# Moving the pieces of the range checks in the second layer of a two-layer attention kernel, and forming the verdict ahead of the last eviction

## The chip, the cores and the metric

The kernel runs as one program on one core of a Trainium2 chip. The metric is the device time of one execution in microseconds (us). Of the kernel before there are three timed runs and one further execution that the hardware profiler recorded.

## The reference, cut to what matters

The input x is an image of 128 rows, 256 columns and 256 channels in float32. Two layers are applied to it, each as a residual on top of a group norm. Layer 0 is a gated row attention with a pair bias. Layer 1, the only one that the change touches, is a banded attention along each row:

```
qkv = x2 @ w_in.T + b_in                       # x2: group norm of x, 128 rows of 256 x 256
scores = einsum('bhid,bhjd->bhij', q, k) / sqrt(64)          # 4 heads of 64
attn = softmax(where(|i - j| <= 16, scores, -inf))
out = einsum('bhij,bhjd->bhid', attn, v)
x = x + out @ w_out.T + b_out
```

The softmax of the kernel is computed without a subtraction of the row maximum: exponentials are summed, and the result is multiplied by the reciprocal of the sum. That is exact enough only while the sums stay in a safe range, so the kernel also looks at its sums, at the exponentials of the pair bias and at the mask, and sets a flag, the verdict. The engines then read the flag, and a slower general kernel would follow if it were set.

## The kernel before, in words

`mixer_kernel` calls `fast_kernel`, loads the verdict into a register of every engine (L2244) and branches on it (L2245). Everything below is the last part of `fast_kernel`, layer 1.

**Tiling.** 128 partitions; a row of the image is 256 positions, two blocks of 128 (NB = 2), and 256 channels are two blocks of 128 (KC = 2). The rows are handled two at a time in 64 objects of class `Pair1` (NP = 64). The order of instructions on every engine is the order in which the Python code is written, since all of it lies in `with tc.manual_schedule()`. Engines run in parallel and wait for one another by semaphores, so the order on each queue is what the change alters.

**The loop.** Iteration p of the loop over 63 pairs (L2115 and after) has four pairs in hand: `was` (pair p-1) is finished, `now` (pair p) goes through its attention, `nxt` (pair p+1) is projected, and `nn` and `n3` are loaded, transposed (`turn`, L1850), normalised (`centre`, L1855) and given the sums and differences of blocks that the projection uses (`differences`, L1868 to L1871, on POOL). The projection is a seven-product scheme: `product(n, i)` for n = 0, 1, 2 (query, key, value) issues the matmuls of product i (L1906, L1902 for the values) into one of two PSUM tiles x and y, ACT copies x to SBUF (L1915, L1913), and `join(n, i)` on DVE (L1922) adds y to that copy. A later product that writes y has to wait until the join before it has read y.

**The attention.** `scores` (PE L1959, ACT exponential L1968, POOL multiplication by the band mask L1970), `apply` (PE L1984 for the values, L1992 for the sums, into the PSUM tiles `o_eo` and `su_y`), `copy_sums` and `copy_odd` (ACT L2003, L2006), `join_sums` and `join_odd` (DVE L2009, L2012), `invert` (DVE reciprocal L2015), `weigh` (DVE L2020), `out_block` (PE L2038, eight matmuls for a row), and `keep_row` (DVE L2046, adds the residual and evicts from PSUM; then the store is issued on SP, L2052 or L2054). `out_row` is `out_block` for both blocks and then `keep_row`. The output tile `y` shares `su_y` with the sums, but for the last pair, where it has its own PSUM tile `ps_y1`.

**The range checks.** `look` puts two pieces on a list. The piece `low` is two DVE instructions, a comparison into the scratch tile `above` (tensor_scalar, L2071) and a minimum over it (tensor_reduce, L2072). The other piece is one DVE instruction, a maximum (tensor_reduce, L2074). `some_checks(n)` takes n pieces from the front of the list `late` if it has any, else of the list `checks`, and issues them at that place of DVE's queue. At p = 1 the list `checks` has 25 looks, that is 50 pieces (16 of the pair bias, one of the mask, eight of layer 0's sums). At p = 58 four looks more are put on it, of layer 1's sums of the first 56 pairs, the last of half width. Each of the last eight pairs (LATE = 8) puts its own two looks on `late` in `weigh`, one for each row.

Pieces are taken at these places of an iteration: **slot 1** after `was.invert(1)` (one piece if p > 0), the **centre slot** after `nn.centre(0)` (two if p > 56), **slot 2** after `now.join_odd(0)` (one if p > 0), and the **end slot** after `n3.turn()` (one if p > 56).

**The end.** After the loop, pair 62 is finished and pair 63 goes through its attention. Two pieces are taken after `now.weigh(0)` of pair 63, the rest at the very end after `now.out_row(1)`. Then follow a comparison of the maxima (`below`, L2081), the minimum over all results (L2231), a matmul with ones that adds it over the partitions (L2233), and the verdict (DVE, L2234).

Of the kernel before, what the change touches and what calls it, by code (L numbers as in the profile page):

```python
# [9 lines left out]
F32 = mybir.dt.float32  # L10
AF = mybir.ActivationFunctionType
ALU = mybir.AluOpType
AX = mybir.AxisListType
# [3 lines left out]
P = 128  # L17
# [756 lines left out]
def fast_kernel(  # L774
# [25 lines left out]
    nc = tc.nc  # L800
# [7 lines left out]
    NB = I // P  # L808
    KC = C // P
    NP = S // 2  # L810
# [10 lines left out]
    ones = const.tile([P, P], F32, name="ones")  # L821
# [109 lines left out]
    for a in range(KC):  # L931
        for h in range(H1):
            n = P // H1
# [5 lines left out]
    for h in range(H1):  # L939
        n = P // H1  # L940
# [10 lines left out]
    ok = const.tile([P, 2, 48], F32, name="ok")  # L951
# [596 lines left out]
    now = nxt = nn = None  # L1548
# [63 lines left out]
    behind, nx, n = None, 0, 0  # L1612
# [41 lines left out]
    with tc.manual_schedule():  # L1654
        old = was = Nobody()
        es = nn3 = None
        for p in range(NP):
# [71 lines left out]
            old, was, now, nxt, nn = was, now, nxt, nn, nn3  # L1729
# [39 lines left out]
    LATE = 8  # L1769
    rsum1 = dram.tile([NP, H1, 2, I], F32, name="rsum1")  # L1770
    with tc.tile_pool(name="l1", bufs=2) as sb, tc.tile_pool(
        name="l1s", bufs=4
    ) as sm, tc.tile_pool(name="ps1_s", bufs=2, space=PSUM) as ps_s, tc.tile_pool(
        name="ps1_o", bufs=1, space=PSUM
    ) as ps_o:

        def mm1(name, side=0):
            return ps_s.tile([P, 512], F32, name=name, tag=f"s{side}")
# [29 lines left out]
        def mix_weights():  # L1808

            a = [[w_in[:, k].rearrange("p (n m c) -> p m n c", n=3, m=KC)[:, m] for k in range(KC)]  # L1810
                 for m in range(KC)]
            s1, s2, s3, s4 = (wst[:, n] for n in range(4))
            nc.gpsimd.tensor_tensor(s1, a[1][0], a[1][1], ALU.add)
            nc.gpsimd.tensor_tensor(s2, s1, a[0][0], ALU.subtract)
            nc.gpsimd.tensor_tensor(s3, a[0][0], a[1][0], ALU.subtract)
            nc.gpsimd.tensor_tensor(s4, a[0][1], s2, ALU.subtract)
# [239 lines left out]
        def pair1(p):  # L2056
            return Pair1(p) if p < NP else Nobody()
# [6 lines left out]
        def look(queue, src, lo):  # L2064

            at = cols[0]
            cols[0] += 1

            def low():
                above = sm.tile([P, I], F32, name="above", tag="above", bufs=1)[:, : src.shape[1]]  # L2070
                nc.vector.tensor_scalar(above, src, lo, None, ALU.is_gt)  # L2071
                nc.vector.tensor_reduce(ok[:, 0, at : at + 1], above, AX.X, ALU.min)  # L2072

            queue += [low, lambda: nc.vector.tensor_reduce(ok[:, 1, at : at + 1], src, AX.X, ALU.max)]  # L2074

        def look_all(src, lo):
            for i in range(0, src.shape[1], I):
                look(checks, src[:, i : min(i + I, src.shape[1])], lo)
# [4 lines left out]
        def some_checks(n):  # L2083
            for _ in range(n):
                queue = late or checks
                if queue:
                    queue.pop(0)()

        def load_sums(src, name):
            t = sb.tile([P, src.shape[0] // P], F32, name=name, tag=name, bufs=1)  # L2090
            nc.sync.dma_start(t, src.rearrange("(a b) -> a b", a=P))
            look_all(t, 1e-16)

        with tc.manual_schedule():
            now, nxt = pair1(0), pair1(1)
            now.turn()
            norm1()
            mix_weights()
            for k in range(KC):
                now.centre(k)  # L2100
            nxt.turn()
            for m in range(KC):
                now.project("qT", m)
                now.project("kT", m)
                nxt.centre(m)
            nxt.differences()
            for r in range(2):
                now.values(r)
            now.add_bias()
            nxt.add_bias()  # L2110
            look_all(eb.rearrange("p h b i -> p (h b i)"), math.exp(-20.0))
            n_eb = cols[0]

            was = Nobody()
            for p in range(NP - 1):  # L2115
                nn = pair1(p + 2) if p == 0 else n3
                n3 = pair1(p + 3)
                if p == 0:
                    nn.turn()
                if p == 1:  # L2120
                    mask_t = sb.tile([S, I], F32, name="mask_all", bufs=1)
                    nc.sync.dma_start(mask_t, mask)
                    look_all(mask_t, 1e-15)
                    n_mask = cols[0]
                    load_sums(rsum.rearrange("n q r c i -> (n q r c i)"), "sums0")
                if p == NP - LATE + 2:
                    load_sums(rsum1[: NP - LATE].rearrange("n q r i -> (n q r i)"), "sums1")

                now.scores(0)
                now.scores(1)  # L2130
                was.apply(1)
                nxt.begin_fast()
                was.copy_sums(1)
                nxt.product(0, 1)
                was.copy_odd(1)
                nxt.product(1, 1)
                was.join_sums(1)
                for n in range(2):
                    nxt.product(n, 2)
                    nxt.join(n, 2)  # L2140
                was.invert(1)
                some_checks(p > 0)
                for i in (6, 5, 7):
                    for n in range(2):
                        nxt.product(n, i)
                for n in range(2):
                    nxt.join(n, 5)
                was.join_odd(1)
                was.weigh(1)
                was.out_row(0)  # L2150
                for n in range(2):
                    nxt.product(n, 4)
                    nxt.product(n, 3)
                    nxt.join(n, 3)
                fast = p < NP - 2
                if fast:
                    nxt.product(2, 1)
                    nxt.product(2, 2)
                    nxt.join(2, 2)
                nn.centre(0)  # L2160
                some_checks(2 if p > NP - LATE else 0)

                now.apply(0)
                now.copy_sums(0)
                if fast:
                    nxt.product(2, 6)
                    nxt.product(2, 5)
                now.copy_odd(0)
                now.join_sums(0)
                was.out_block(1, 0)  # L2170
                if fast:
                    nxt.product(2, 7)
                now.join_odd(0)
                some_checks(p > 0)
                was.out_block(1, 1)
                if fast:
                    nxt.join(2, 5)
                was.keep_row(1)
                if fast:
                    nxt.product(2, 4)  # L2180
                    nxt.product(2, 3)
                    nxt.join(2, 3)
                now.invert(0)
                now.weigh(0)
                nn.centre(1)
                nn.differences()
                nn.add_bias()
                n3.turn()
                some_checks(p > NP - LATE)
                if p == NP // 2:  # L2190
                    below(0, n_eb, math.exp(20.0))
                    below(n_eb, n_mask, 1e15)
                was, now, nxt = now, nxt, nn

            now.scores(0)
            was.apply(1)
            was.copy_sums(1)
            was.copy_odd(1)
            now.values(0)
            was.join_sums(1)  # L2200
            was.join_odd(1)
            was.invert(1)
            was.weigh(1)
            was.out_row(0)
            now.scores(1)
            now.values(1, 1)
            was.out_row(1)
            now.apply(0)
            now.copy_sums(0)
            now.copy_odd(0)  # L2210
            now.join_sums(0)
            now.join_odd(0)
            now.invert(0)
            now.weigh(0)
            some_checks(2)
            now.apply(1)
            now.copy_sums(1)
            now.copy_odd(1)
            for b in range(NB):
                now.out_block(0, b)  # L2220
            now.join_sums(1)
            now.invert(1)
            now.join_odd(1)
            now.weigh(1)
            now.keep_row(0)
            now.out_row(1)
            some_checks(len(checks) + len(late))
            below(n_mask, cols[0], 1e8)

        tot = sm.tile([P, 1], F32, name="okmin", bufs=1)  # L2230
        nc.vector.tensor_reduce(tot, ok.rearrange("p a n -> p (a n)"), AX.X, ALU.min)  # L2231
        ps = mm1("ok_ps")
        nc.tensor.matmul(ps[:, 0:1], ones, tot, start=True, stop=True)  # L2233
        nc.vector.tensor_scalar(verdict, ps[0:1, 0:1], P - 0.5, None, ALU.is_lt)  # L2234


# [63 lines left out]
```

## Time and profile before

| what | value |
|---|---|
| three timed runs | 3146.48, 3148.49, 3148.63 us (median 3148.49) |
| the profiled execution's own time | 3147.36 us |
| its span, first to last instruction | 3145.6 us |
| mean TensorE clock granted | 0.983 of full speed |
| busy share of the span | PE 96%, DVE 77%, POOL 72%, ACT 50% |
| layer 1's loop, first scores of p = 0 to first scores of p = 62 | 2007.19 to 3093.58 us |
| verdict written, span's end | 3139.03 us, 3145.6 us |

How to read the lines that follow: a line of the timeline gives the start in us from the span's beginning, the time from the start to the end of the merged instructions, the engine, the source line, the operation, output and inputs by the program's names, the shapes, how many instructions were merged, and in brackets how long the engine sat idle before and what ended that. PE is the matmul stream, PEld the weight loads beside it, SPq the queue of SyncE that issues DMAs.

### The profile page before, as it was taken

To read this page: it belongs to the slowest core of one execution; us is meant where nothing else is said; L and a number is where in the kernel's file an instruction comes from. 1 tells how busy PE (TensorE), PEld (TensorE's weight loads), DVE (VectorE), ACT (ScalarE), POOL (GpSimd) and SP (SyncE) were. 2 spreads that over 40 slices of the span, in tenths; PEclk is the share of its full clock that TensorE was granted. 3 is DMA by queue.
4 is the path that set the end of the run, shared out by engine and by line. 5 is a ranking of instruction groups with operands and counts; after the bars stand their busy time and mean duration, and the time that the engine had idled before them with its cause. 6 is when DMAs were issued, how large, how long until landed. Compare 5 with 4: busy or idle time off the path is not lost.

```text
span 3145.6 us, 80608 instructions
## 1 busy us (share of the span) xinstructions
PE 3020.1 (96%) x33630; PEld 2099.2 (67%) x33630; DVE 2406.7 (77%) x4007; ACT 1573.3 (50%) x2637; POOL 2270.8 (72%) x1633
## 2 busy tenths in 40 slices
PE   5679999999999999999999999899999999999997
PEld 3345555665555556655555565688888888888886
DVE  7976777777777777777777777688888777777787
ACT  3454444444444444444444444355555555555553
POOL 3459898898889988888899887455555555555552
PEclk9789999999999999999999999999999999999998
DMA  9952334323333343333333332534344444444441
GB/s 358 389 174 56 97 70 99 99 64 92 94 99 70 98 99 73 89 91 94 72 96 98 88 82 65 119 91 94 92 94 92 94 92 94 92 93 92 93 98 36
DMA packets 690951, 328.17 MB, mean 104 GB/s; under 512 B 538672, under 2 KB 639920, under 8 KB 689424
## 3 DMA queue, kind: packets, MB, share of 16 engines
q1 hardware_dynamic: 686176, 320.28, 39.5%
q8 instruction: 266, 4.36, 0.6%
q10 hardware_dynamic: 4400, 2.63, 0.3%
q14 instruction: 109, 0.89, 0.1%
HBM read 254.09 MB, written 68.75 MB: 103 GB/s over the span
## 4 chain that ended last, share of the span: by engine, by line
PE 84%; DVE 8%; DMA 2%; issue 2%; POOL 2%; ACT 1%; ACTq 0%; DVEq 0%; POOLq 0%; SPq 0%
PE ps_p L1347 21%; PE ps_sc L1384 8%; PE ps_qk L1906 8%; PE ps_ov L1419 7%; PE ps_y L1474 7%; PE ps_v L1365 7%; PE ps_qk L1902 7%; PE ps_su_y L2038 6%; PE ps_o L1984 3%; PE ps_su L1427 3%; PE ps_sc L1959 3%; PE ps_su_y L1992 2%; DVE rv L2015 2%; DMA xa<-in_x_dram 1%; DVE st L1182 1%
## 5 line engine op out<-in xcount | busy, mean ns | idle before, releaser
L1408 POOL TENSOR_TENSOR eboth<-e 128x512 f32<-128x512 f32 x512 | 745.0, 1476 | 177.3 <-PE ps_su L1427 96.2
L1404 DVE TENSOR_TENSOR e<-ps_sc,eb 128x1024 f32<-128x1024 f32 x384 | 458.4, 1221 | 289.3 <-ACT ps_sc L1396 289.2
L1396 ACT ACTIVATE ps_sc<-ps_sc 128x1024 f32<-128x1024 f32 x384 | 375.7, 1008 | 435.9 <-PE ps_sc L1384 309.7
L1384 PE MATMUL ps_sc<-qT,kT 32*128 32x256 f32 x4096 | 294.1, 400 | 0.9 <-DVE e L1404 0.9
L1869 POOL TENSOR_TENSOR dT<-xgT,dT 128x256 f32<-128x256 f32 x63 | 45.9, 729 | 317.4 <-ACT xgT L1855 317.4
L1970 POOL TENSOR_TENSOR e<-e,bw 128x384 f32<-128x384 f32 x256 | 249.5, 1003 | 11.3 <-ACT e L1968 11.3
L2038 PE MATMUL ps_su_y<-w_out,oT 128*128 128x256 f32 x1008 | 254.5, 385 | 1.8 <-DVE sums L2009 1.8
L1384 PEld LDWEIGHTS ps_sc<-qT,kT 32*128 32x128 f32 x4096 | 185.3, 184 | 103.0 <-issue 91.0
L1474 PEld LDWEIGHTS ps_y<-wo,oT 128*128 128x128 f32 x1024 | 194.1, 190 | 83.9 <-issue 44.5
L1347 PE MATMUL ps_p<-xnT,wq 128*128 128x512 f32 x512 | 247.6, 606 | 0.8 <-POOL xnT L1334 0.8
L1419 PE MATMUL ps_ov<-e,v 128*32 128x256 f32 x4096 | 247.6, 382 | 0.0
L1347 PE MATMUL ps_p<-xgT,wg 128*128 128x512 f32 x512 | 247.2, 605 | 0.1
L1474 PE MATMUL ps_y<-wo,oT 128*128 128x256 f32 x1024 | 242.3, 380 | 3.5 <-POOL oT L1464 2.7
L1365 PE MATMUL ps_v<-wv,xnT 128*128 128x256 f32 x1024 | 242.0, 379 | 1.6 <-ACT xgT L1316 1.6
L1347 PE MATMUL ps_p<-xnT,wk 128*128 128x512 f32 x512 | 240.6, 592 | 0.0
L1365 PEld LDWEIGHTS ps_v<-wv,xnT 128*128 128x128 f32 x1024 | 194.5, 190 | 55.9 <-issue 31.1
L1915 ACT ACTIVATE u<-ps_qk,bin_c 128x256 f32<-128x256 f32 x378 | 174.5, 476 | 102.2 <-PE ps_qk L1906 102.2
L2015 DVE RECIPROCAL rv<-sums 128x256 f32<-128x256 f32 x128 | 223.1, 1743 | 0.0
L2038 PEld LDWEIGHTS ps_su_y<-w_out,oT 128*128 128x128 f32 x1008 | 181.7, 190 | 23.6 <-DVE sums L2009 2.6
L1419 PEld LDWEIGHTS ps_ov<-e,v 128*32 128x32 f32 x4096 | 120.0, 109 | 108.4 <-issue 41.8
L1906 PE MATMUL ps_qk<-dT,wst 128*128 128x256 f32 x756 | 174.8, 380 | 7.1 <-DVE qT L1922 7.1
L1868 POOL TENSOR_TENSOR dT<-xgT 128x256 f32<-128x256 f32 x63 | 45.9, 729 | 186.0 <-ACT xgT L1855 186.0
(231 smaller groups left out, 6546.4 us busy)
## 6 DMA issues: line engine op xcount, KB each, us to landing
xa<-in_x_dram SPq DMA_DIRECT2D x8, 4096.0 KB
xt<-in_x_dram SPq DMA_DIRECT2D x64, 512.0 KB
x<-xo SPq DMA_DIRECT2D x16, 2048.0 KB
xt<-x SPq DMA_DIRECT2D x64, 512.0 KB
rvb<-rsum SPq DMA_DIRECT2D x252, 128.0 KB
xs<-x SPq DMA_DIRECT2D x252, 128.0 KB
out_dram<-yo SPq DMA_DIRECT2D x63, 512.0 KB
xs<-in_x_dram SPq DMA_DIRECT2D x248, 128.0 KB
```

Source lines behind the costliest of these rows:

```text
L1347: nc.tensor.matmul(ps, w[:, k, m * P : (m + 1) * P], getattr(self, src)[:, k, :], start=(k == 0), stop=(k == KC - 1),)
L1365: nc.tensor.matmul(self.ps_v[:, b * C : (b + 1) * C], self.xnT[:, k, t * P : (t + 1) * P], wv[:, k, :], start=(k == 0), stop=(k == KC - 1),)
L1384: nc.tensor.matmul(self.pss[q // 2][:, q % 2, b, :], self.kT[rs, c, r * I + b * P : r * I + (b + 1) * P], self.qT[rs, c, r * I : (r + 1) * I],
L1396: nc.scalar.activation(self.pss[a], ps, AF.Exp)
L1404: nc.vector.tensor_tensor(es[a], pss[a], eb[:, h : h + 2], ALU.mult)
L1408: nc.gpsimd.tensor_tensor(t, es[a][:, :, 0, :], es[a][:, :, 1, :], ALU.add)
L1419: nc.tensor.matmul(ov[q * D0 : (q + 1) * D0, c, :], self.v[:, r, b, h * D0 : (h + 1) * D0], es[q // 2][:, q % 2, b, :], start=(b == 0), st ...
L1474: nc.tensor.matmul(self.ps_y[:, b * C : (b + 1) * C], self.oT[r][:, k, b * P : (b + 1) * P], wo[:, k, :], start=(k == 0), stop=(k == KC - 1),)
L1906: nc.tensor.matmul(to, lhs, rhs, start=start, stop=True, skip_group_check=True)
L1970: nc.gpsimd.tensor_tensor(e[:, q], e[:, q], bcast(bw.rearrange("p b w -> p (b w)"), 1, KC), ALU.mult)
L2015: nc.vector.reciprocal(self.rv[:, r, :], self.sums)
L2038: nc.tensor.matmul(self.y[:, b], self.oT[r][:, k, b * P : (b + 1) * P], w_out[:, k, :], start=(k == 0), stop=(k == KC - 1),)
```

## The change

It does five things. (1) `look` puts the maximum ahead of `low` on the list. (2) The end slot is removed, and slot 2 takes two pieces in place of one in the iterations with p > 56. (3) After the loop, six pieces are taken right after `was.out_row(0)` of pair 62, and the two after `now.weigh(0)` of pair 63 are not. (4) At the end `now.out_row(1)` is split: the remaining pieces, `below` and the minimum over all results stand ahead of the last row's `out_block` calls in the code, so that DVE has them in its queue between `keep_row(0)` and `keep_row(1)`. (5) The matmul of the verdict follows the last row's matmuls directly on PE, ahead of `keep_row(1)`; the verdict itself stays last on DVE. No computation is left out: the same looks are taken in all.

```diff
-            queue += [low, lambda: nc.vector.tensor_reduce(ok[:, 1, at : at + 1], src, AX.X, ALU.max)]
+            queue += [lambda: nc.vector.tensor_reduce(ok[:, 1, at : at + 1], src, AX.X, ALU.max), low]
...
                 now.join_odd(0)
-                some_checks(p > 0)
+                some_checks(2 if p > NP - LATE else p > 0)
                 was.out_block(1, 1)
...
                 n3.turn()
-                some_checks(p > NP - LATE)
                 if p == NP // 2:
...
             was.out_row(0)
+            some_checks(6)
             now.scores(1)
...
             now.weigh(0)
-            some_checks(2)
             now.apply(1)
...
             now.keep_row(0)
-            now.out_row(1)
             some_checks(len(checks) + len(late))
             below(n_mask, cols[0], 1e8)
-
-        tot = sm.tile([P, 1], F32, name="okmin", bufs=1)
-        nc.vector.tensor_reduce(tot, ok.rearrange("p a n -> p (a n)"), AX.X, ALU.min)
-        ps = mm1("ok_ps")
-        nc.tensor.matmul(ps[:, 0:1], ones, tot, start=True, stop=True)
+            tot = sm.tile([P, 1], F32, name="okmin", bufs=1)
+            nc.vector.tensor_reduce(tot, ok.rearrange("p a n -> p (a n)"), AX.X, ALU.min)
+            for b in range(NB):
+                now.out_block(1, b)
+            ps = mm1("ok_ps")
+            nc.tensor.matmul(ps[:, 0:1], ones, tot, start=True, stop=True)
+            now.keep_row(1)
         nc.vector.tensor_scalar(verdict, ps[0:1, 0:1], P - 0.5, None, ALU.is_lt)
```

## The prediction

> **What bounds the kernel now.** I read the page first, then the pairs of layer 1 one by one in the timeline, then the tail. The page's first line and the shares of the chain:
>
> ```profile
> PE 3020.1 (96%) x33630; PEld 2099.2 (67%) x33630; DVE 2406.7 (77%) x4007; ACT 1573.3 (50%) x2637; POOL 2270.8 (72%) x1633
> ...
> PE 84%; DVE 8%; DMA 2%; issue 2%; POOL 2%; ACT 1%; ACTq 0%; DVEq 0%; POOLq 0%; SPq 0%
> ```
>
> PE bounds the kernel. A DVE instruction costs time only where PE waits for it, so I looked for those places. The starts of the first score matmuls (L1959) give each pair's period: 17.50 us for p = 1 to 25, where pieces are taken (437.92 us for the 25, with a few larger ones), and 17.375 us where none are; p = 57 takes 17.50, p = 58 to 61 take 18.95 each. So a pair with pieces loses 0.125 us and a late pair 1.58 us. The timeline of p = 60 shows why:
>
> ```profile
> 3058.50 1.24 DVE L1850 STREAM_TRANSPOSE xT<-xs 128x1024 f32<-128x1024 f32 x1
> ...
> 3059.13 2.36 POOL L1861 TENSOR_TENSOR xt<-xt,bout_r 128x1024 f32<-128x1024 f32 x1
> ...
> 3059.66 1.98 DVE L2071 TENSOR_SCALAR above<-rv 128x256 f32<-128x256 f32 x1
> ...
> 3062.02 0.41 DVE L2009 TENSOR_TENSOR sums<-ps_su_y,sums 128x256 f32<-128x256 f32 x1
> 3062.35 0.41 DVE L1922 TENSOR_TENSOR qT<-ps_qk,u 128x256 f32<-128x256 f32 x1
> ...
> 3062.82 1.99 PE L1906 MATMUL ps_qk<-dT,wst 128*128 128x256 f32 x8 [1.53 <-DVE qT L1922]
> ```
>
> The `low` of the end slot of p = 59 runs behind the transpose, takes 1.98 us while POOL adds the bias, pushes the join of qT back, and PE idles 1.53 us.
>
> In slot 1 a `low` meets POOL's mask multiplications:
>
> ```profile
> 2325.48 3.92 POOL L1970 TENSOR_TENSOR e<-e,bw 128x384 f32<-128x384 f32 x4
> 2326.55 1.02 DVE L2071 TENSOR_SCALAR above<-sums 128x256 f32<-128x256 f32 x1
> ...
> 2327.61 0.42 DVE L2072 TENSOR_REDUCE ok<-above 128x1 f32<-128x256 f32 x1
> 2327.95 0.41 DVE L1922 TENSOR_TENSOR qT<-ps_qk,u 128x256 f32<-128x256 f32 x1
> ```
>
> In slot 2, where POOL is idle for 4.87 us, the same comparison takes 0.28 us, and the value join that follows starts 0.41 us after the start of ACT's copy of u, against 0.40 us with a maximum there: it waits for ACT either way.
>
> ```profile
> 3072.62 0.28 DVE L2071 TENSOR_SCALAR above<-sums 128x256 f32<-128x256 f32 x1
> ...
> 3072.94 0.42 DVE L2072 TENSOR_REDUCE ok<-above 128x1 f32<-128x256 f32 x1
> ...
> 3073.38 0.42 DVE L1922 TENSOR_TENSOR v<-ps_qk,u 128x256 f32<-128x256 f32 x1
> ...
> 3074.09 0.61 PE L1902 MATMUL ps_qk<-wst,xgT 128*128 128x128 f32 x4
> ```
>
> The tail, where nothing overlaps from one pair to the next:
>
> ```profile
> 3111.62 1.08 DVE L2071 TENSOR_SCALAR above<-rv 128x256 f32<-128x256 f32 x1
> ...
> 3113.08 0.41 DVE L2009 TENSOR_TENSOR sums<-ps_su_y,sums 128x256 f32<-128x256 f32 x1
> ...
> 3125.58 3.75 PE L2038 MATMUL ps_y<-w_out,oT 128*128 128x256 f32 x8 [1.04 <-DVE oT L2020]
> ...
> 3129.86 3.78 PE L2038 MATMUL ps_y<-w_out,oT 128*128 128x256 f32 x8 [0.53 <-DVE oT L2020]
> ...
> 3133.68 0.69 DVE L2046 TENSOR_TENSOR yo<-ps_y,xt 128x512 f32<-128x512 f32 x1 [3.27 <-PE ps_y L2038]
> ...
> 3138.28 0.56 PE L2233 MATMUL ok_ps<-okmin,ones 128*128 128x1 f32 x2 [4.64 <-DVE okmin L2231]
> 3138.88 0.15 DVE L2234 TENSOR_SCALAR verdict<-ok_ps 1x1 int32<-1x1 f32 x1 [0.74 <-PE ok_ps L2233]
> ```
>
> Behind the last eviction DVE works through eight pieces (3134.29 to 3137.66) before PE may add up. From the verdict's start to the span's end are 6.72 us.
>
> **What the Trainium skill says.** "SBUF — State Buffer", section "SBUF: two separate sides": DVE and GpSimd (POOL) share a pair of ports as an exclusive lock; a DVE operation in a two-port mode blocks, or is blocked, for a whole instruction. "VectorE: DVE Perf Modes", section "The perf-mode tier table": tensor_scalar in float32 from SBUF runs in such a mode, tensor_reduce never does. The trace agrees: L2071 takes 0.28 us alone, 1.02 beside L1970 and 1.98 beside L1861, L2072 and L2074 stay near 0.42. "TensorE: Matmul & The Clock Gate", section "What's actually happening": the clock halves after a window of idleness, and the windows run free. The trace has the clock at 0.5 from 3124.7 us on, which is why eight L2038 take 3.75 us there and 1.99 before. "Runtime: NRT & Kernel Launch", section "Instruction fetch mechanics": a taken branch makes the engine fetch its next page by DMA. PE's branch at L2245 takes 3.90 us, the others' about 0.05.
>
> **The change, part by part.** DVE's spacing is below its duration: a maximum takes 0.33 us of the queue, an undisturbed `low` 0.31 + 0.34 = 0.65.
>
> (1) *Order swapped, p = 1 to 25 and p = 57.* Slot 1 gets the maximum, slot 2 the `low`. In slot 1 the maximum ends within the 0.51 us that the next join waits for ACT in a pair without pieces: no cost. In slot 2 the `low` ends at 16.03 us into the pair, the join is due at 16.14: no cost, covered by ACT's copy; were POOL in the way, it would be 0.7 to 1.7 us more. So these pairs go to 17.375: 26 x 0.125 = **3.25 us** gained.
>
> (2) *End slot removed.* p = 58 to 61 lose their stall: 4 x (18.953 - 17.376) = **6.31** gained. At p = 62 PE did not wait for it. In slot 2 there are now the pair's own `low` and a piece of the old sums, a maximum at p = 58, 60, 62 and a `low` at 59 and 61 (at 57 there is no second piece yet). From 15.38 us into the pair they end at 16.36 or 16.68; the join of v (0.42 us) then ends at 16.80 or 17.12 in place of 16.56, and PE's product that writes the same tile is due at 16.84. With 0.05 us for the signal (as L2009 to L2038): a stall of 0.0 or 0.33, so 2 x 0.33 = **0.66** lost. In the centre slot `low` now comes first; it would start 0.08 us ahead of POOL's L1868 and take the ports. If POOL wins, each late pair loses some 0.3; I take none.
>
> (3) *First `low` of the tail gone.* The join of sums at 3113.08 moves to 3111.62; L2038 then follows its predecessor at the spacing of the next such couple (3116.29 to 3118.12: 1.83), at 3112.45 rather than 3113.55: **1.10** gained. *Six pieces after `out_row(0)`.* DVE evicts at about 3114.91 and is free at 3115.51. Three maxima and three `low` are 3 x 0.98 = 2.94 us, so 3118.5, plus up to 1.0 where one meets POOL's two multiplications (3115.94 to 3117.9). PE brings the next row at 3118.95. Queued behind them is `keep_row(1)`, and behind that PE's sums of the last pair: 0 to 0.5 lost, I take **0.3**.
>
> (4) *Two pieces after `weigh(0)` of pair 63 gone.* Between 3125.35 and 3126.33 they held up `join_sums(1)`; that is 0.98 us of DVE, but now PE is late next: its first eight matmuls at half clock, spaced 3.41 us, let the last row start at 3124.48 + 3.41 = 3127.9, and oT is ready at 3127.8. Before it was 3129.86, of which 1.10 is counted: **0.86** gained.
>
> (5) *Verdict ahead of the last eviction.* The last row's matmuls end at 3127.9 + 3.78 = 3131.7. Meanwhile DVE evicts the row before (3128.27, 0.6 us) and does five pieces (2.42 us), `below` 0.22 and the minimum 0.27: 3131.8. The verdict's matmul starts at about 3131.9, the verdict 0.6 later, at 3132.5, with `keep_row(1)` (0.61 us from 3131.72 on) done ahead of it. Before it was 3138.88: 6.38 in all, less 1.96 counted, is **4.42** gained. The last store of 256 KB is issued only some 0.05 us before the verdict, not 4.4 us. In the trace such a store is on the wires for about 1.2 us, 0.8 us after its issue: just when PE fetches its instructions. This collision was not there before; between 0 and 1.2 us, I take **0.5** lost. It lands well before the 6.72 us are over.
>
> Sum: 3.25 + 6.31 - 0.66 + 1.10 - 0.3 + 0.86 + 4.42 - 0.5 = 14.48 us. The profiled execution took 3147.36, so 3132.9. That is 1.13 below the median shown; the four executions of before spread over 2.15 us with a mean of 3147.74, and from that mean I get **3133.3**.
>
> **Rivals.**
>
> *A, the stalls move.* The late pairs keep 0.3 in the centre slot and 0.33 in slot 2 each (5 x 0.63 = 3.2 in place of 0.66), the six pieces cost 0.5 and the fetch 1.2. Then 11.0 us, 3136.7. For it: DVE is continuously busy around slot 2; against: POOL idles there.
>
> *B, the clock stays full at the end.* With the windows falling otherwise, the last 16 matmuls take 2 x 1.9 us rather than 2 x 3.75. `keep_row(0)` no longer waits, but the five pieces then bound the verdict: oT at 3127.8, eviction to 3128.4, pieces, `below` and minimum to 3131.3, so only 0.5 sooner, and if the idle gaps before shrink too, up to 2: 3131.3 to 3132.8. Before had the slow clock in its profile; nothing in the code fixes it.
>
> *C, nothing to be measured.* The verdict's path isn't the end: had the store or the barrier bounded the span, (5) and (4) were hidden (5.3), and a stall like that of the end slot came back in slot 2 of the late pairs (6.3). Then 14.5 - 11.6, about 3145. Against it: after 3136.5 no data moves but small packets.
>
> *D, slower.* The swapped `low` collides with POOL in slot 2 of 26 pairs as it did with L1861: 1.98 rather than 0.28 makes the join of v 1.6 us late, PE's slack of 0.23 gone: 1.36 x 26 = 35 us lost, 3169. It decides against the change from a comparison of about 1.1 us there (14.5 / 26 = 0.56, plus slack 0.23 and the spare 0.11 and 0.28 itself). Against it: POOL is idle from 13.2 to 17.9 us into the pair.
>
> **How the numbers follow.** A difference of about 0.2%, 6.3 us, is what a measurement of this kernel can tell from no change. Forecast 0.70, A 0.13, B 0.08, C 0.05, D 0.04. Faster by over 0.2%: 0.70 + 0.13 + 0.08 = 0.91; within: 0.05; slower: 0.04. The range takes in the unknown costs (0 to 1.0 in the centre, 0 to 0.5, 0 to 1.2), the spread of 2.15 us between executions and A and B: 3129.8 to 3138.0.
>
> **What would show it.** Right: all pairs from p = 6 to 58 at 17.375 (apart from the few that are longer now too), p = 59 and 61 at about 17.7; L2071 in slot 2 at 0.28; no PE wait for qT in p = 58 to 61; L2233 directly behind L2038; L2234 about 14 us earlier. Wrong: L2071 over 1 us in slot 2, a PE wait for the join of v in the early pairs, or a span whose end stands over 7.5 us behind the verdict.

## The result, and the profile after

Five runs of the changed kernel have a median of 3133.77 us (3132.93 to 3136.62), five of the kernel before 3148.63 us (3146.48 to 3150.12). The ratio is 0.9954, with a 95% interval of 0.9942 to 0.9965: faster by 11 to 18 us. Forecast were 3133.3 us, with a range of 3129.8 to 3138.0.

The changed kernel's page: the first line, and the chain that ended last. Its span is 3132.0 us.

```profile
PE 3016.0 (96%) x33630; PEld 2099.4 (67%) x33630; DVE 2398.5 (77%) x4007; ACT 1574.1 (50%) x2637; POOL 2268.7 (72%) x1633
...
PE 90%; DVE 3%; DMA 3%; POOL 2%; issue 2%; ACT 0%; SPq 0%; ACTq 0%; POOLq 0%; DVEq 0%
```

The busy times hardly move, and DVE has the same 4007 instructions. What moves is the chain: DVE's share falls from 8% to 3%. Most of the work that PE used to wait for is now done where PE does not wait.

The same places in the timeline, first a late pair (p = 58), with the columns start, length, engine, line, operation, output and inputs. At the place of the end slot the transpose is followed directly by the joins:

```profile
3019.62 1.24 DVE L1850 STREAM_TRANSPOSE xT<-xs 128x1024 f32<-128x1024 f32 x1
...
3020.78 0.38 DVE L2009 TENSOR_TENSOR sums<-ps_su_y,sums 128x256 f32<-128x256 f32 x1
3021.22 0.42 DVE L1922 TENSOR_TENSOR qT<-ps_qk,u 128x256 f32<-128x256 f32 x1
3021.38 2.75 PE L1906 MATMUL ps_qk<-dT,wst 128*128 128x256 f32 x12
```

PE's twelve products run without a gap; before there was one of 1.53 us in them. Slot 2 of the next pair, p = 59, is the one with two `low` pieces:

```profile
3049.49 0.28 DVE L2071 TENSOR_SCALAR above<-rv 128x256 f32<-128x256 f32 x1
...
3049.81 0.42 DVE L2072 TENSOR_REDUCE ok<-above 128x1 f32<-128x256 f32 x1
...
3050.26 0.29 DVE L2071 TENSOR_SCALAR above<-sums 128x256 f32<-128x256 f32 x1
...
3050.92 0.41 DVE L1922 TENSOR_TENSOR v<-ps_qk,u 128x256 f32<-128x256 f32 x1
...
3051.39 0.71 PE L1902 MATMUL ps_qk<-wst,xgT 128*128 128x128 f32 x4 [0.28 <-DVE v L1922]
```

The comparisons take 0.28 and 0.29 us, and the join of v comes late enough that PE waits 0.28 us for it, by the route that the prediction named. The end of the kernel:

```profile
3121.03 0.68 DVE L2046 TENSOR_TENSOR yo<-ps_y,xt 128x512 f32<-128x512 f32 x1
3121.17 1.99 PE L2038 MATMUL ps_y<-w_out,oT 128*128 128x256 f32 x8 [1.33 <-DVE oT L2020]
...
3124.38 0.25 DVE L2228 TENSOR_REDUCE okmin<-ok 128x1 f32<-128x96 f32 x1
3124.55 0.68 DVE L2046 TENSOR_TENSOR yo<-ps_y,xt 128x512 f32<-128x512 f32 x1
3124.78 0.35 PE L2232 MATMUL ok_ps<-okmin,ones 128*128 128x1 f32 x2 [1.61 <-DVE okmin L2228]
3125.17 0.15 DVE L2234 TENSOR_SCALAR verdict<-ok_ps 1x1 int32<-1x1 f32 x1
```

The pieces lie beside the last row's matmuls, and the eviction beside the verdict's matmul. One thing differs from the forecast: the last row's eight matmuls take 1.99 us, not 3.78, because the TensorE clock is at full here until 3127.0 us. So PE is done at 3123.16 and waits 1.61 us for DVE's minimum; the verdict's matmul does not follow directly, as the prediction said it would.

By stages, each from one profiled execution of the two kernels (starts of the first score matmuls, and the verdict):

| stage | before, us | after, us | gained |
|---|---|---|---|
| span's start to the loop | 2007.19 | 2008.96 | -1.77 |
| p = 1 to 25 | 437.92 | 435.43 | 2.49 |
| p = 26 to 56 | 540.58 | 540.42 | 0.16 |
| p = 57 | 17.50 | 17.38 | 0.12 |
| p = 58 to 61 | 75.82 | 70.29 | 5.53 |
| p = 62 to the verdict's start | 45.30 | 38.10 | 7.20 |
| verdict's start to the span's end | 6.72 | 6.83 | -0.11 |

With p = 0 (14.57 and 14.59) the sum is 13.6, the difference of the spans. The first row lies ahead of everything that was changed; the starts of the loop vary between 2006.9 and 2009.3 us over the profiles of this study, so it is no effect of the change.

### The profile page after: what moved, and what is told of

Its sections match the earlier page's. It is cut to its first block, busy times and chain, and to the rows that moved or that the text cites. A ratio compares the mean times of both kernels' runs of the same rounds, so it can differ in the third digit from the quotient of the medians.

```text
span 3132.0 us, 80583 instructions
## 1 busy us (share of the span) xinstructions
PE 3016.0 (96%) x33630; PEld 2099.4 (67%) x33630; DVE 2398.5 (77%) x4007; ACT 1574.1 (50%) x2637; POOL 2268.7 (72%) x1633
## 4 chain that ended last, share of the span: by engine, by line
PE 90%; DVE 3%; DMA 3%; POOL 2%; issue 2%; ACT 0%; SPq 0%; ACTq 0%; POOLq 0%; DVEq 0%
PE ps_p L1347 21%; PE ps_qk L1906 13%; PE ps_sc L1384 8%; PE ps_ov L1419 7%; PE ps_su_y L2038 7%; PE ps_qk L1902 7%; PE ps_y L1474 7%; PE ps_v L1365 7%; PE ps_o L1984 4%; PE ps_su L1427 3%; PE ps_sc L1959 3%; PE ps_su_y L1992 2%; DMA xa<-in_x_dram 1%; DVE st L1182 1%; DVE zst L1104 1%
## 5 line engine op out<-in xcount | busy, mean ns | idle before, releaser
L1970 POOL TENSOR_TENSOR e<-e,bw 128x384 f32<-128x384 f32 x256 | 248.0, 1000 | 10.7 <-ACT e L1968 10.7
L1347 PEld LDWEIGHTS ps_p<-xnT,wk 128*128 128x128 f32 x512 | 97.4, 190 | 122.4 <-issue 122.4
L1868 POOL TENSOR_TENSOR dT<-xgT 128x256 f32<-128x256 f32 x63 | 45.9, 728 | 182.8 <-ACT xgT L1855 182.8
```

The lines of the kernel that those rows point to most:

```text
L1347: nc.tensor.matmul(ps, w[:, k, m * P : (m + 1) * P], getattr(self, src)[:, k, :], start=(k == 0), stop=(k == KC - 1),)
L1970: nc.gpsimd.tensor_tensor(e[:, q], e[:, q], bcast(bw.rearrange("p b w -> p (b w)"), 1, KC), ALU.mult)
```

## The experiments

Two theories stood against each other. **P**: a piece costs what it makes DVE late beyond the slack at its place, and a `low` is slow only where its comparison meets POOL. **Q**: pieces cost by their number and place, the end slot above all, whatever is in them. The first four kernels make parts of the change alone. For e1 and e2 the number to look at is the pair's period, for e3 and e4 the time from the start of p = 62 to the verdict. Numbers of parts are from here on those of the prediction, which at the end differ from the list of the change: (3) of that list makes the gains of the prediction's (3) and (4), save for the first `low` of the tail, and (4) and (5) of the list together are the prediction's (5).

### e1: part (1) alone

```diff
-            queue += [low, lambda: nc.vector.tensor_reduce(ok[:, 1, at : at + 1], src, AX.X, ALU.max)]
+            queue += [lambda: nc.vector.tensor_reduce(ok[:, 1, at : at + 1], src, AX.X, ALU.max), low]
```

> The kernel before with part (1) alone: the maximum ahead of `low` on the list; all slots stay where they were. Theory P (a piece costs what it delays DVE beyond the slack at its place, and `low` is slow only beside POOL): pairs 1 to 25 and 57 go to 17.375 (about 3 us), and, beyond what the prediction counted, the end slot of p = 57 to 61 now holds a maximum of 0.33 us instead of a `low` of 2.3 us, while the slack there is 2.34 - 1.53 = 0.81, so the late pairs lose their stall too and keep only the 0.125 of a `low` in slot 1: 4 x 1.45 = 5.8; the tail gains 1.1 since the piece at its head is a maximum. Some 10 us in all. Rival Q (the end slot costs by its place, whatever piece is in it): late pairs stay at 18.95, 3 us in all.

Measured: 3140.85 us (3138.67 to 3142.17), ratio 0.9971 (0.996 to 0.9983), that is 8.2 us by the medians. Pairs 1 to 25 are at 17.38, apart from the few that the last section tells of, and p = 58 to 61 at 17.50 to 17.52, not at 18.95. DVE's timeline in a late pair of e1:

```profile
3055.38 1.24 DVE L1850 STREAM_TRANSPOSE xT<-xs 128x1024 f32<-128x1024 f32 x1
3056.54 0.38 DVE L2074 TENSOR_REDUCE ok<-rv 128x1 f32<-128x256 f32 x1
3056.84 0.41 DVE L2009 TENSOR_TENSOR sums<-ps_su_y,sums 128x256 f32<-128x256 f32 x1
3057.17 0.41 DVE L1922 TENSOR_TENSOR qT<-ps_qk,u 128x256 f32<-128x256 f32 x1
```

There is still a piece in the end slot, but it is a maximum and takes 0.30 us of the queue in place of 2.35. Q is refuted: the place alone costs PE nothing, as long as the piece there is short. And the order alone takes away the stall that the prediction gave to part (2).

### e2: part (2) alone

```diff
                 now.join_odd(0)
-                some_checks(p > 0)
+                some_checks(2 if p > NP - LATE else p > 0)
...
                 n3.turn()
-                some_checks(p > NP - LATE)
```

> The kernel before with part (2) alone: end slot removed, slot 2 takes two pieces in the late pairs, order `low` then maximum as before. Theory P: pairs 1 to 25 stay at 17.50; late pairs go to 17.50 to 17.6 (the `low` in slot 1 keeps its 0.125, slot 2 gets a maximum and another piece), 5.7 us; the tail gains 1.1 at its head and loses 0.3 to 0.7 by one piece more at the end. About 6.4 us. Rival Q gives the same here; with e1 it is told apart. If both e1 and e2 take the stall away, (1) and (2) are not additive.

Measured: 3143.35 us (3140.97 to 3146.98), ratio 0.9982 (0.9972 to 0.9991), 5.7 us by the medians. Pairs 1 to 25 stay at 17.49 to 17.52, apart from the same few; p = 58 to 61 take 17.60, 17.43, 17.60 and 17.43. So (1) and (2) each remove the late pairs' stall, and what they gain does not add.

### e3: part (5) alone

The edit is the last hunk of the diff of the change, on the kernel before: the last pieces and the minimum ahead of the last row, and the verdict's matmul ahead of the last eviction.

> The kernel before with part (5) alone: last pieces, `below` and the minimum ahead of the last row's matmuls in DVE's queue, the verdict's matmul directly behind them, the last eviction after. Theory P: eight pieces of 3.37 us start at 3130.3 instead of 3134.3, so the verdict comes about 3.9 us sooner, less 0 to 1 us for the store that is issued as the branch fetches: 3 to 3.9 us faster. Rival R (the last store or the barrier sets the end): no change within 0.5 us, the time from the verdict to the span's end grows by what the verdict gains.

Measured: 3146.05 us (3144.02 to 3149.19), ratio 0.999 (0.9984 to 0.9997), 3.0 us by the medians. From the start of p = 62 to the verdict it is 41.12 us instead of 45.30, and 6.9 instead of 6.72 from there to the end. The end's path did lead through the verdict, and R is refuted; the time after the verdict grows by 0.2, not by what was gained, and over all profiles of this study it varies from 6.7 to 7.2 us. The end of e3:

```profile
3131.55 3.52 PE L2038 MATMUL ps_y<-w_out,oT 128*128 128x256 f32 x8 [2.32 <-DVE oT L2020]
...
3135.77 0.68 DVE L2046 TENSOR_TENSOR yo<-ps_y,xt 128x512 f32<-128x512 f32 x1
3136.00 0.35 PE L2233 MATMUL ok_ps<-okmin,ones 128*128 128x1 f32 x2 [0.94 <-DVE okmin L2229]
```

### e4: the six pieces alone

```diff
             was.out_row(0)
+            some_checks(6)
             now.scores(1)
...
             now.weigh(0)
-            some_checks(2)
```

> The kernel before with the six pieces after pair 62's first row, and without the two after pair 63's weigh(0); the rest as before. Theory P: the end has four pieces instead of eight (1.4 us less), the join of sums of pair 63 comes 0.98 us sooner, of which 0.5 to 1.0 reaches the last row's matmuls depending on whether the TensorE clock is at half then; 0 to 0.5 us are lost where the six pieces hold up keep_row(1). About 2 us faster. Rival: the six pieces block keep_row(1), and with it the sums of the last pair, by as much as they save: no change.

Measured: 3145.33 us (3143.51 to 3147.69), ratio 0.9987 (0.9981 to 0.9994), 3.8 us by the medians. The profile has 41.22 us from p = 62 to the verdict, 4.08 less than before, and of this 1.79 is the clock: the last row's matmuls take 1.99 us here and 3.78 before. The rest is 0.98 from the join of sums and 1.30 from the shorter list at the end: 2.3, near the 2 that were expected. The six pieces held up nobody: the eviction behind them starts at 3123.57, as soon as PE's row is there.

The four medians' gains add up to 20.7 us, the whole change gained 14.9. The 5.8 between are what is counted twice: e1 and e2 both lose the late stall (5.8 us for p = 58 to 61) and the 1.1 us at the head of the tail. That makes 6.9, and the medians are not exact enough to tell it from 5.8.

### e5: a `low` that does not share ports with POOL

```diff
-                above = sm.tile([P, I], F32, name="above", tag="above", bufs=1)[:, : src.shape[1]]
-                nc.vector.tensor_scalar(above, src, lo, None, ALU.is_gt)
-                nc.vector.tensor_reduce(ok[:, 0, at : at + 1], above, AX.X, ALU.min)
+                above = sm.tile([P, I], F32, name="above", tag="above", bufs=1)[:, :1]
+                nc.vector.tensor_reduce(above, src, AX.X, ALU.min)
+                nc.vector.tensor_reduce(ok[:, 0, at : at + 1], src, AX.X, ALU.min)
...
             below(n_mask, cols[0], 1e8)
+            for a, b, lo in ((0, n_eb, math.exp(-20.0)), (n_eb, n_mask, 1e-15), (n_mask, cols[0], 1e-16)):
+                nc.vector.tensor_scalar(ok[:, 0, a:b], ok[:, 0, a:b], lo, None, ALU.is_gt)
```

> The kernel before, all slots and the order as they were, but `low` is two minima (tensor_reduce, 0.33 us of DVE's queue each) instead of a comparison and a minimum; the comparison is made once at the end on the 48 result columns (three small instructions more there, 0.6 us). DVE's own work in a piece is the same 0.65 us; only the instruction that shares ports with POOL is gone. Theory P (lock): in the end slot 0.66 is below the slack of 0.81, so the late pairs drop from 18.95 to 17.38 to 17.5, and pairs 1 to 25 from 17.50 to about 17.38 to 17.45; with 0.8 at the head of the tail some 8 to 9 us faster. Rival Q (it is the number of pieces and their place, not POOL): late pairs stay near 18.9, pairs 1 to 25 at 17.50, within 1 us of before.

Measured: 3138.93 us (3137.31 to 3139.3), ratio 0.9969 (0.9956 to 0.9981), 9.9 us faster with every piece where it was before. All late pairs are at 17.38 to 17.39, and so are pairs 1 to 25, with the same exceptions. A late pair of e5, at the end slot:

```profile
3053.36 1.24 DVE L1850 STREAM_TRANSPOSE xT<-xs 128x1024 f32<-128x1024 f32 x1
3054.52 0.38 DVE L2071 TENSOR_REDUCE above<-rv 128x1 f32<-128x256 f32 x1
3054.82 0.41 DVE L2072 TENSOR_REDUCE ok<-rv 128x1 f32<-128x256 f32 x1
3055.14 0.41 DVE L2009 TENSOR_TENSOR sums<-ps_su_y,sums 128x256 f32<-128x256 f32 x1
```

This is the sharpest of the runs. Place and number of pieces are those of before, the two instructions take 0.62 us of the queue instead of 2.35, and PE waits for nothing. So the lock on the shared ports, which the Trainium skill describes in "SBUF — State Buffer", section "SBUF: two separate sides", is what made `low` dear: it accounts for 1.7 of the 2.35 us.

e5 also changes how much the first instruction writes (128x1 instead of 128x256), so the volume of the write is a rival. Against it, the join L1922, one of whose inputs lies in PSUM, writes 128x256 in at most 0.43 us, beside POOL as alone, in the profiles of before and of e6. And the slow comparisons have the mark of a lock: all 187 of 128x256 that took over 0.35 us in the twelve profiles end 0.15 to 0.16 us after the end of a POOL instruction.

### e6: POOL kept busy over slot 2

```diff
                 now.join_sums(0)
+                busy = sm.tile([P, 4, I], F32, name="busy", tag="busy", bufs=1)
+                nc.gpsimd.tensor_tensor(busy, bcast(now.sums, 1, 4), bcast(now.sums, 1, 4), ALU.add)
                 was.out_block(1, 0)
```

> The changed kernel with one POOL instruction more in each iteration of the loop (128x1024, sums read twice, the result unused), placed so that it runs from about 14.1 to 16.5 us into the pair, over slot 2. Theory P: the comparison in slot 2 waits for it and takes about 1.1 us instead of 0.28; the join of v ends at 17.4 where PE needs it at 16.84: pairs 1 to 25 go from 17.38 to about 17.9 to 18.0 (14 us), pairs 57 to 61 lose about 1 us each, pairs 26 to 56, which have the same POOL instruction and no piece, stay at 17.375. About 19 us slower than the changed kernel, slower than before. If the ports did not matter, or if PE did not wait for that join: nothing in pairs 1 to 25 either. If the POOL instruction itself were the cost, pairs 26 to 56 would be longer too.

Measured: 3144.42 us (3142.92 to 3147.79), 10.7 us more than the changed kernel's median, and still faster than before (0.9988, 0.9979 to 0.9996). The size was missed. The pairs 26 to 56 went to 17.42 (0.05 for the POOL instruction itself), pairs 1 to 25 to 17.50, and p = 57 to 61 took 91.20 us together, 3.5 more than in the changed kernel. Slot 2 of one of the early pairs of e6:

```profile
2284.82 1.90 POOL L2171 TENSOR_TENSOR busy<-sums 128x1024 f32<-128x1024 f32 x1 [4.64 <-DVE sums L2009]
2285.40 0.69 DVE L2012 TENSOR_TENSOR odd<-ps_o,odd 128x512 f32<-128x512 f32 x1 [0.66 <-ACT odd L2006]
...
2286.01 0.85 DVE L2071 TENSOR_SCALAR above<-eb 128x256 f32<-128x256 f32 x1
...
2287.24 0.41 DVE L1922 TENSOR_TENSOR v<-ps_qk,u 128x256 f32<-128x256 f32 x1
```

The comparison waited (0.85 us instead of 0.28), but the POOL instruction took 1.90 us where I had put 2.4, and slot 2 began at 15.16 us into the pair, 0.2 earlier than in the changed kernel. The join was 0.26 us late, and the slack there took most of it up. In the late pairs, where a second piece follows, it did not: PE waits for that join 0.35 us at p = 58 and 60 and 0.80 us at p = 59 and 61. Another 1.02 us at p = 60 have nothing to do with slot 2: PE waits there for qT, since `weigh` (L2020, both inputs in SBUF) runs beside POOL's L1861 and takes 2.57 us instead of 0.69. So the added POOL instruction also shifts other collisions, and e6 is not a clean test of slot 2 in the late pairs. What was forecast as rival D exists, but one collision of 0.57 us is not enough for it.

### e7: two small repairs

```diff
                 some_checks(2 if p > NP - LATE else p > 0)
+                if p == NP // 2:
+                    below(0, n_eb, math.exp(20.0))
+                    below(n_eb, n_mask, 1e15)
...
                     load_sums(rsum1[: NP - LATE].rearrange("n q r i -> (n q r i)"), "sums1")
+                    checks[:] = checks[::2] + checks[1::2]
```

with the same three lines taken out at the end of the iteration.

> The changed kernel with two things more: the two comparisons of maxima at p = 32 (`below`) move from the end of the iteration to slot 2, and of layer 1's older sums the maxima are taken before the `low` pieces, so that slot 2 of p = 58 to 61 always has `low` and a maximum. Theory P: the pair at p = 32, 18.44 us, goes to 17.38 (1.06 gained, since POOL is idle there); p = 59 and 61 go from 17.79 to 17.46 (0.7 gained); the tail has a `low` in place of a maximum among the six pieces and loses up to 0.4. About 1.3 us faster than the changed kernel, too little for the times to show, visible in the pairs.

Measured: 3132.76 us (3131.89 to 3134.69), ratio to before 0.995 (0.9937 to 0.9964). The period of p = 33, which begins right behind the old place of `below`, is 17.38 us instead of the changed kernel's 18.44 (the expectation names it by the iteration, p = 32), and p = 57 to 61 take 86.73 together, five times 17.35. Against the changed kernel the median is 1.0 lower; the runs of the two overlap, so only the pairs show the gain.

### e8: part (2) undone in the changed kernel

The edit is that of e2, taken back.

> The changed kernel with part (2) undone: one piece in slot 2, one in the end slot, the order swapped as in the changed kernel. Theory P, after the runs of the parts alone: with the order swapped the end slot holds a maximum, so (2) is not needed: p = 58 to 61 take 17.51 each (70.05 us for the four, against 70.29 in the changed kernel), and the end has a piece less. Within 1 us of the changed kernel. If (2) were what removes the stall, the late pairs would go back to 18.95, 6 us slower than the changed kernel.

Measured: 3133.71 us (3132.49 to 3136.82), ratio to before 0.9955 (0.9942 to 0.9969). p = 58 to 61 take 17.49 to 17.52 each, 70.02 us together against 70.29. Part (2) is of no use beside part (1).

### e9: one minimum for a `low`

On e7, `low` becomes one minimum, and `below` compares both columns:

```diff
...
-                nc.vector.tensor_scalar(above, src, lo, None, ALU.is_gt)
-                nc.vector.tensor_reduce(ok[:, 0, at : at + 1], above, AX.X, ALU.min)
+                nc.vector.tensor_reduce(ok[:, 0, at : at + 1], src, AX.X, ALU.min)
...
+            nc.vector.tensor_scalar(ok[:, 0, start:stop], ok[:, 0, start:stop], lo, None, ALU.is_gt)
```

> The version of e7 with `low` as one minimum (tensor_reduce, 0.33 us of the queue) instead of a comparison and a minimum; the comparison with the lower bounds is made on the result columns, beside those of the maxima (a not-a-number in the data is then left to what the minimum makes of it, which the comparison before would have caught). Theory P: no piece meets POOL or lasts over 0.33 us; p = 58 to 61 go from 17.46 or less to 17.38, the five pieces at the end take 1.6 instead of 2.4 us, so PE no longer waits 0.9 us for the minimum over all results. One to 1.5 us faster than e7, some 17 us faster than before. Rival: the end is bound by the last row's matmuls and eviction by now, no change against e7 within 0.3 us in the profile from p = 62 to the verdict.

Measured: 3133.62 us (3129.84 to 3135.55), ratio to before 0.9954 (0.994 to 0.9968). In the profile p = 62 to the verdict takes 37.27 us (38.10 in the changed kernel, 39.9 in e7, whose profile has the clock at half for most of the last two rows), and the span is 3128.1, the shortest of all. PE still waits 0.79 us for the minimum over all results. The gain is in the profile and not in the median: the runs spread over 5.7 us. As a faster version it is inconclusive.

### e10: part (4) undone

Two of the six pieces go back to their old place, after `weigh(0)` of pair 63.

```diff
             was.out_row(0)
-            some_checks(6)
+            some_checks(4)
...
             now.weigh(0)
+            some_checks(2)
             now.apply(1)
```

> The changed kernel with part (4) undone: four pieces after pair 62's first row, two again after weigh(0) of pair 63, the rest at the end. Theory P: the join of sums of pair 63 comes 0.98 us later, and with the TensorE clock at full the last row is bound by oT, so the whole 0.98 reaches the verdict, not the 0.86 that the prediction took from a clock at half; PE idles 2.3 us ahead of the last row instead of 1.3. If the clock halves in that idle time, as in the profiles of e1 to e3, the last row's eight matmuls take 3.3 to 3.6 us instead of 2.0 and 0.5 to 1.5 us more are lost. From the start of p = 62 to the verdict 39.1 to 40.6 us against 38.1 in the changed kernel. If the clock falls out by chance alone, this profile may have it at full: then 39.1.

Measured: 3135.04 us (3133.17 to 3136.06), ratio to before 0.9956 (0.9942 to 0.9969). The median is 1.3 us above that of the changed kernel, but the runs of the two overlap, so the profile has to decide. From p = 62 to the verdict it takes 39.2 us, against 38.10. The last row's start and its matmuls in e10:

```profile
3121.98 3.36 PE L2038 MATMUL ps_y<-w_out,oT 128*128 128x256 f32 x8 [2.32 <-DVE oT L2020]
...
3125.07 0.25 DVE L2229 TENSOR_REDUCE okmin<-ok 128x1 f32<-128x96 f32 x1
...
3126.05 0.15 DVE L2235 TENSOR_SCALAR verdict<-ok_ps 1x1 int32<-1x1 f32 x1
```

The idle time ahead of the last row is back at 2.32 us, and the clock was at half for most of the row. By the starts, the last row is 0.98 us later than in the changed kernel (35.08 us after p = 62 instead of 34.10), as the theory has it.

## Why the prediction was right, point by point

**The bound and the mechanism: right.** PE bounds the kernel, and DVE's pieces cost only where PE waited for DVE. e5 shows that the lock makes `low` dear, e1 that its place does not. What it had wrong is to which edit the largest gain belongs, as (2) says.

**(1), 3.25 us: measured 2.61** (2.49 for p = 1 to 25, 0.12 for p = 57). The pairs go to 17.375 as said. The 0.6 that is missing lies in p = 1, which takes 17.71 us as before, and in p = 4, 7 and 10, which take 17.6; at p = 7 the weight loads pause for 0.34 us without any releaser in the trace, so it is no wait for DVE (see the last section). What the prediction overlooked is that the order also settles what the end slot holds.

**(2), 6.31 - 0.66 = 5.65: measured 5.53** for the sum, but the attribution failed. The step "p = 58 to 61 lose their stall" is credited to the removed end slot; e1 and e8 show that the swap alone does it, and that (2) then makes the four pairs 0.27 us longer. That the sum fits all the same is owed to both edits being in the change: e1 and e2 show that either of them removes the stall. The stalls of slot 2 were named rightly and sized at 0.0 and 0.33; PE waits 0.28 us for v at p = 59 and 61. The four pairs are at 17.46, 17.80, 17.26 and 17.78, together 0.79 over four times 17.375, where 0.66 were forecast. The race in the centre slot went as assumed: at p = 58 the comparison starts at 3029.13 and takes 0.28, POOL's L1868 starts at 3029.23 and takes 0.77 instead of 0.73.

**(3), 1.10 - 0.3: measured 1.09 and no loss.** The tail's first row starts 18.88 us after p = 62 instead of 19.97. Only one of the six pieces' comparisons met POOL for long (0.52 us), and DVE was free just when PE had the next row.

Another 0.11 us, which no term named, is gained up to the next to last row.

**(4), 0.86: measured 0.98.** The term assumed the clock at half, with PE late next. At full clock oT is late next, and all of DVE's time counts; e4 and e10 both give 0.98.

**(5), 4.42 - 0.5: measured 5.02 - 0.11.** Two sizes were off. From the last row's start to the verdict 4.6 us were forecast and 4.00 measured: with the clock at full DVE starts its pieces about 0.5 us sooner, since the eviction ahead of them does not wait for PE. And the store that was to fall into the instruction fetch costs little: its data moves from 3125.9 to 3127.1 us. The fetch that the prediction assumed is there, but only from 3126.9 us on, when the first packets of the instruction queues move, so the two hardly meet. PE's branch takes 3.64 us, and 3.62 to 3.84 in all kernels with the store there, against 3.38 to 3.90 in those without; SyncE's load of the verdict starts at 3125.7 instead of 3125.4, because the store is issued first on its queue. That 0.3 is all that can be seen of the collision, and the 0.11 is within what the time after the verdict varies.

**The rivals.** A was wrong about the centre slot and the fetch, and right that slot 2 costs a little more. B, the full clock, is what the profile of the changed kernel happens to have. C is refuted by e3, D did not happen, and e6 shows that a collision of 0.57 us in slot 2 would not have brought it about. The total came out closer than the terms, and that is luck: (1) was too high by 0.6, and the terms of the end, (3) to (5), too low by 1.5, partly the clock's doing.

## What to carry to other kernels

Price an instruction on DVE by what POOL does at that moment, and by the slack behind it: the same comparison cost 0.28, 1.0 or 2.0 us, and PE felt it only beyond what the next join could wait. The pieces are not alone in this: `weigh` took 0.69 us or up to 1.3 in the kernels before and after, and each of the slow ones ends 0.55 us after a POOL instruction does. When work is taken from lists in turn, a change of the order changes what every slot gets, so go through the queue slot by slot before a gain is given to one of two edits. At the end of a kernel, let the last engine's small work lie beside the last matmuls, and ask which chain, the store or the flag, the end really waits for.

## What the runs showed of the hardware that was not expected

Some pairs are longer in most profiles, whatever the kernel: p = 4, 7, 10, 41, 44 and 47 take 17.4 to 18.5 us where their neighbours take 17.38 or 17.50. In the pair at p = 10 of e2 (18.46 us), the weight loads:

```profile
2184.85 0.14 PEld L1992 LDWEIGHTS ps_su_y<-e,ones 64*32 64x32 f32 x3 [0.88 <-issue]
```

PE's weight loads stop for 0.88 us with nothing that they wait for in the trace. The traces hold a trail, though. One DMA queue, q8, carries instructions, with 2.3 packets a pair; PE has 595 instructions a pair, no other engine over 30, so they are PE's. All 54 stops of over 0.31 us of this kind in the loops of the twelve profiles end 1.2 to 1.6 us after such a packet has landed, and the packets come 3.5 to 11.9 us apart. So PE waited there for instructions, as far as times can tell; no run changed their supply, and why it is late at these places stays open. These gaps add up to a few us and are part of the spread of the runs.

The clock of TensorE halved within the last row, or up to 0.3 us ahead of it, in all five profiles where PE had idled 2.3 us before that row (e1, e2, e3, e5 and e10; the eight matmuls took 2.5 to 3.6 us), and stayed at full there in the changed kernel, e4 and e9, where it had idled 1.3. But in the kernel before both of the last two rows ran at half, with 1.04 and 0.53 us of idle time ahead of them; so did the row before the last and most of the last in e6 and e7, with 0.7 and 1.0 us ahead of the first of the two and none between them, and part of the row before the last in e8, so the length of one gap does not decide it. What does was not settled; for the last row it is worth 1.8 us here.
